# The last attention of a four-layer network begun among the last steps of the stage before it

## The chip, the cores and the metric

The kernel runs on one core of one Trainium2 chip. Its time is the device time of one execution in microseconds (us), given as the median of several runs. A profiled execution, taken separately, gives the trace from which single instructions are read.

The engines are named as in the profile: PE is TensorE (matrix products and transposes), PEld its weight loads, DVE is VectorE, ACT is ScalarE, POOL is GpSimd, and SP is SyncE, which here issues the DMAs. Every engine works through its own instructions in order; semaphores hold an instruction until what it needs is there. PSUM, in which TensorE leaves its results, has eight banks.

## The reference, cut to what matters

A tensor x of 16 tiles of 128 rows by 256 columns passes through four layers. Each layer adds an attention over a context (2048 rows) and then a feed-forward, each on the layer-normed x:

```python
x = x + L0_xattn(layernorm(x), ctx);        x = x + L0_ffn(layernorm(x))   # experts
x = x + L1_xattn(layernorm(x), ctx, mask);  x = x + L1_ffn(layernorm(x))   # ternary weights
x = x + L2_xattn(layernorm(x), ctx);        x = x + L2_ffn(layernorm(x))   # top four of 64 routes
x = x + L3_xattn(layernorm(x), ctx);        x = x + L3_ffn(layernorm(x))   # experts
```

The two parts that the change touches are these:

```python
def L2_ffn(x, A, B, W, bias):
    vecs = einsum('arh,bsh->bsar', A, x)             # 64 vectors of 16 per row
    routes = one_hot(top4(norm(vecs))).sum(-2) / 4
    v = einsum('bsa,bsar->bsr', routes, vecs)
    return x @ W.T + bias + einsum('bsa,ajr,bsr->bsj', routes, B, v)

def L3_xattn(x, cond, Wq, bq, Wkv, bkv, Wp, bp):      # 16 heads of 16
    q = (x @ Wq + bq) / 4;  k, v = split(cond @ Wkv + bkv)
    q, k, v = int8_roundtrip(q), int8_roundtrip(k), int8_roundtrip(v)
    attn = uint8_roundtrip(softmax(q @ k.T))          # over all 2048 rows of the context
    return (attn @ v) @ Wp + bp
```

## The kernel before, in words

`run` has four stages: the loading of x, the first layer (`l0`), the middle, and the last layer (`l3`).

**The middle** does layers 1 and 2, and the keys and values of layer 3, tile by tile. Each piece of work on one tile is a Python generator that yields between its steps: `l1_xattn`, `l1_ffn`, `l2_xattn`, `l2_ffn`, `l3_keys`, `l3_values`. The dictionary `starts` says at which step a generator begins (for tile t: 4t, 4t + 3, 4t + 7, 4t + 16, 4t + 2; the values at 4), and `side_by_side` advances all live generators in turn. The engines' final instruction order is made from this by the framework's scheduler.

Each generator belongs to a *stream*, which sets the buffers and the PSUM tag that its matrix products use. The middle's eight banks are e = 1, w = 3, x = 2, av = 1, f = 1. Layer 1 (streams `s1x`, `s1f`) takes tag e; layer 2's feed-forward (`s2f`) takes f, and so do keys and values (`s3`); layer 2's attention (`s2x`) takes x. With one bank behind e or f, each user waits until the one before it has been read out.

The steps of `l2_ffn`, whose last two tiles (14 and 15) end the middle: the layernorm (L187 to L193), its transpose (L213, copied at L229), `vecs` (L237, eight matmuls into two banks of tag w), their squares (L762, L763), the top four (L765 to L771), z and v (L776 to L781), the transposes of z (L213, L221), `out` (L237, 4 + 16 matmuls), and the addition to x (L787).

**The last layer** is a `tc.manual_schedule`: the order on every engine is the order in which the code stands. A unit u is one head of one tile, 256 in all. For each unit, `scores` makes four pieces of 128x512 (L933), `peak` their maxima (L939), `bias` the exponent's bias (L944, L945), and `exponentials` four exponentials into p (L955), after which SP issues one DMA that transposes p (L959); four units later (LAG) `values` multiplies it with the values (L967). Three buffers hold p (pool `l3p`), five its transpose. Scores of the units u + 1 and u + 2 are made while u is exponentiated.

Work per tile hangs on the dictionary `steps`, counted from the tile's first unit: steps below zero prepare the next tile's queries (`stats`, `norm` L982, `turn_h` L988 and L990, `project_q` L1001, `quant_q` L1008 to L1018, `turn_q` L1025 to L1028), those from 20 on finish attention and run the feed-forward of ten experts. For tile 0 the steps below zero stand ahead of the loop. The quantised queries of a tile lie in one of two buffers `qTs`, block-diagonal by pairs of heads, whose zeros a memset lays at the start (L1162). `take` gives each product the bank that came free first, `give` returns it; at the start they are taken b0, b1 and so on in order.

Between the two, `moe_weights` loads the weights of the last feed-forward (`w_L_ffn_wgu` 3520 KB at L95, `w_L_ffn_wd` in two parts at L384 and L386, `w_L_ffn_gateT` at L95). SP issues them, as it does all transposes of p. `l3_weights`, called before the middle, makes the pool w3, which stays to the end; buffers are laid out in memory in the order in which pools are opened and tiles asked for, so what is loaded later may lie over what an earlier stage still reads, and then waits for it.

Of the kernel before, what the change touches and what calls it, by code (L numbers as in the profile page):

```python
# [18 lines left out]
F32 = mybir.dt.float32  # L19
BF16 = mybir.dt.bfloat16  # L20
# [5 lines left out]
ALU = mybir.AluOpType  # L26
AX = mybir.AxisListType
PSUM = bass.MemoryType.PSUM

P = 128  # L30
NT = 16
D = 256
NH = 16
T = NT * P

MAGIC = 12582912.0
# [4 lines left out]
class Net:  # L41
# [767 lines left out]
    def l3_weights(self):  # L809

        w = {n: self.load(f"L3_xattn_{k}", [P, 2, D], f"x3{n}", "(c p) n -> p c n", p=P)
             for n, k in (("q", "Wq"), ("o", "Wp"))}
        w["qb"], w["ob"] = self.rows("L3_xattn_bq", "x3qb"), self.rows("L3_xattn_bp", "x3ob")
        w["k"] = [self.w.tile([P, 8, T // 2], BF16, name=f"kst{j}", tag=f"kst{j}") for j in range(2)]
        w["v"] = self.w.tile([P, NT, D], BF16, name="v_int", tag="v_int")
        w["sv"] = self.w.tile([P, 2], F32, name="sv", tag="sv")
        return w

    def l3_kv_weights(self):
# [28 lines left out]
    def l3_values(self, w, w3, pool):  # L848
# [18 lines left out]
        for j in range(8):  # L867
# [8 lines left out]
                nc.tensor.transpose(ps[:, i, :], vi[:, i, :], self.identb)  # L876
            nc.scalar.copy(w3["v"][:, t:t + 4, oc * P:(oc + 1) * P], ps)

    def middle(self, w3):

        self.tag = "e"
        w1f = self.w1f
        with (self.psum(e=1, w=3, x=2, av=1, f=1), self.stream("x1", bufs=1, small=2, tag="e", side="right") as s1x,
              self.stream("f1", bufs=1, small=2, tag="e", side="right") as s1f, self.pool("w2", 1) as self.w,
              self.stream("kv", bufs=1, small=2, tag="f") as s3, self.stream("x", bufs=1, small=2) as s2x,
              self.stream("f", bufs=1, small=2) as s2f):
            w2x, w2f, w3k = self.l2_xattn_weights(), self.l2_ffn_weights(), self.l3_kv_weights()
            starts = {}
            for t in range(NT):
                for step, st, make in ((0, s1x, lambda p, t=t: self.l1_xattn(t, p)),  # L890
                                       (3, s1f, lambda p, t=t: self.l1_ffn(t, w1f, p)),
                                       (7, s2x, lambda p, t=t: self.l2_xattn(t, w2x, p)),
                                       (16, s2f, lambda p, t=t: self.l2_ffn(t, w2f, p)),
                                       (2, s3, lambda p, t=t: self.l3_keys(t, w3k, w3, p))):
                    starts.setdefault(4 * t + step, []).append((st, make))
            starts[4].append((s3, lambda p: self.l3_values(w3k, w3, p)))
            self.side_by_side(starts)
        self.tag, self.small = None, self.small0

    def l3(self, w3, moe_w):  # L900
# [7 lines left out]
        nc, tc = self.nc, self.tc  # L908
        qw, ow, qb, ob, kst, v, sv = (w3[n] for n in ("q", "o", "qb", "ob", "k", "v", "sv"))
# [4 lines left out]
        with (self.pool("l3x", bufs=2) as pool, self.pool("l3p", bufs=3) as pp,  # L914
              self.pool("l3t", bufs=LAG + 1) as tp, self.pool("l3m", bufs=1) as mp,
              self.pool("l3e", bufs=3) as ep):
            st = {}

            banks = {f"b{j}": float(j - 7) for j in range(7)}

# [9 lines left out]
            def scores(u, q):  # L930
                t, hd = divmod(u, NH)
                ps, tag = st["s", u, q] = take([P, 512], "piece")
                nc.tensor.matmul(ps, qTs[t % 2][:, hd, :],  # L933
                                 kst[q // 2][:, hd // 2, 512 * (q % 2):512 * (q % 2) + 512], start=True, stop=True)

            def peak(u, q):
                if q == 0:
                    st["nm", u] = self.s(4, "nm")
                nc.vector.tensor_reduce(st["nm", u][:, q:q + 1], st["s", u, q][0], AX.X, ALU.max, negate=True)  # L939

            def bias(u):
                t, hd = divmod(u, NH)
                nb = st["nb", u] = self.s(1, "nb")
                nc.vector.tensor_reduce(nb, st.pop(("nm", u)), AX.X, ALU.min)  # L944
                nc.vector.tensor_scalar(nb, nb, st["sq", t][:, hd:hd + 1], LN255, ALU.mult, ALU.add)  # L945

            def exponentials(u):
                t, hd = divmod(u, NH)
                if hd == 0:
                    st["z", t] = pool.tile([P, NH, 4], F32, name="z", tag="z")  # L950

                p, nb = pp.tile([P, T], I16, name="p", tag="p"), st.pop(("nb", u))
                for q in range(4):
                    ps, tag = st.pop(("s", u, q))
                    nc.scalar.activation(p[:, 512 * q:512 * q + 512], ps, AF.Exp, bias=nb,  # L955
                                         scale=st["sq", t][:, hd:hd + 1], accum_out=st["z", t][:, hd, q:q + 1])
                    give(tag, u + 0.2 * (q + 1))
                pT = st["pT", u] = tp.tile([P, NT, P], I16, name="pT", tag="pT")
                nc.sync.dma_start_transpose(pT, p)  # L959

            def values(u):
                t, hd = divmod(u, NH)
                if hd == 0:
                    st["av", t] = self.bank([P, NH, 16], "av", "av")
                pb = st.pop(("pT", u)).bitcast(F16)
                for c in range(NT):
                    nc.tensor.matmul(st["av", t][:, hd, :], pb[:, c, :], v[:, c, hd * 16:(hd + 1) * 16],  # L967
                                     start=(c == 0), stop=(c == NT - 1))
# [159 lines left out]
            def down(k):  # L1128
                def step(t, u):
# [7 lines left out]
                    if k == 3:  # L1137
# [6 lines left out]
            steps = {-16: [stats], -15: [norm], -14: [turn_h], -13: [project_q], -12: [quant_q], -6: [turn_q],  # L1144
                     20: [divide], 21: [turn_o], 22: [project_o],
                     23: [stats_m], 24: [norm_m], 25: [turn_m], 27: [logits], 28: [top], 29: [combine]}
# [6 lines left out]

            N = NT * NH
            act = mp.tile([P, 14 * P], F32, name="act", tag="act")


            qTs = [mp.tile([P, NH, P], BF16, name=f"qT{j}", tag=f"qT{j}") for j in range(2)]
            with tc.manual_schedule(engines={E.PE, E.DVE, E.Activation, E.Pool, E.SP}):
                nc.gpsimd.memset(act[:, NE * IN:], 0.0)  # L1160
                for qT in qTs:
                    nc.gpsimd.memset(qT, 0.0)  # L1162
                for n in sorted(n for n in steps if n < 0):
                    for f in steps[n]:
                        f(0, -1)
                for q in range(4):
                    scores(0, q)
                    peak(0, q)
                bias(0)
                for q in range(2):  # L1170
                    scores(1, q)
                    peak(1, q)
                for u in range(N + 29):
                    if u < N:
                        exponentials(u)
                    if u + 1 < N:
                        for q in (2, 3):
                            scores(u + 1, q)
                            peak(u + 1, q)
                        bias(u + 1)  # L1180
                    later = []
                    for t in range(NT):
                        for f in steps.get(u - NH * t, ()) if u - NH * t >= 0 or t > 0 else ():
                            later.append(f(t, u))
                    if 0 <= u - LAG < N:
                        values(u - LAG)
                    for q in range(2):
                        if u + 2 < N:
                            scores(u + 2, q)
                    if u + 2 < N:  # L1190
                        peak(u + 2, 0)
                    for f in later:
                        if f:
                            f()
                    if u + 2 < N:
                        peak(u + 2, 1)
# [83 lines left out]
```

## Time and profile before

| what | value |
|---|---|
| median of 3 runs | 2981.75 us (2979.78 to 2983.23) |
| profiled execution: its time | 2974.05 us |
| its span in the trace | 2972.3 us |
| granted TensorE clock, mean | 0.931 |
| busy share PE, DVE, ACT, POOL | 82%, 66%, 59%, 34% |
| first layer, by the trace | up to about 1148 us |
| middle | about 1148 to 1827 us |
| last layer's first exponential | 1841.31 us |

The profiled execution's time holds 1.75 us that lie around the span. Times in the timeline are counted from the span's start; a row gives start, length, engine, line, operation, and in brackets how long the engine was idle before and what ended that. PEclk is the granted share of TensorE's full clock. Busy shares over the whole span mix four stages that have different limits, so a change at one place has to be read from the rows of that place.

### The profile page before, as it was taken

Reading aid. Unit: us, or ns where it says so; the run is one execution under the profiler, and the core shown is the slowest. Engines: PE = TensorE matmul, PEld = TensorE weight load, DVE = VectorE, ACT = ScalarE, POOL = GpSimd, SP = SyncE. Lnnn points to the kernel's source line nnn. Section 1 sums busy time; section 2 is a strip of 40 time slices with the busy share of each in tenths; the row PEclk is TensorE's granted clock in tenths of the full one; section 3 lists DMA queues with packets and bytes.
Section 4 is the critical chain, followed back from the end, with each engine's and each line's share of the span. In section 5 each row is a group of like instructions: output and inputs, shape, how many; then the busy total and the mean of one; then the engine's idle time right before and its main releaser. Section 6 shows DMA issues by size and latency. Waiting matters only on the chain. (4 is left out here: it accounts for less than half of the span.)

```text
span 2972.3 us, 41664 instructions
## 1 busy us (share of the span) xinstructions
PE 2438.9 (82%) x14053; PEld 1544.4 (52%) x14070; DVE 1958.2 (66%) x5045; ACT 1753.9 (59%) x4636; POOL 997.9 (34%) x1587
## 2 busy tenths in 40 slices
PE   4789999999999877788888885777777777777778
PEld 2456666666666544455555552344444444444445
DVE  2455566665666634577666644987877887877874
ACT  1234444444444432555555542988888888888884
POOL 2444444444443322555555531111111111121101
PEclk9999999999999998999999996699998999999999
DMA  5000000000000011000000003876666666666662
GB/s 208 1 1 1 1 1 1 1 1 1 1 1 36 23 44 32 5 5 5 5 5 5 1 1 99 155 132 121 126 123 123 123 124 123 128 124 118 125 124 56
DMA packets 559830, 171.38 MB, mean 58 GB/s; under 512 B 538912, under 2 KB 555904, under 8 KB 558848
## 3 DMA queue, kind: packets, MB, share of 16 engines
q1 hardware_dynamic: 559616, 168.72, 28.0%
q8 instruction: 111, 1.82, 0.2%
q14 instruction: 103, 0.84, 0.1%
HBM read 32.37 MB, written 2.10 MB: 12 GB/s over the span
## 5 line engine op out<-in xcount | busy, mean ns | idle before, releaser
L955 ACT ACTIVATE p<-piece,nb,hs 128x512 int16<-128x512 f32 x1024 | 785.2, 791 | 27.4 <-issue 17.2
L939 DVE TENSOR_REDUCE nm<-piece 128x1 f32<-128x512 f32 x1024 | 651.9, 683 | 111.0 <-PE piece L933 103.1
L933 PE MATMUL piece<-kst,qT 128*128 128x512 bf16 x1023 | 368.0, 415 | 201.4 <-DVE ma L1116 88.4
L1117 POOL TENSOR_TENSOR act<-ma,mb 128x176 f32<-128x176 f32 x160 | 88.9, 557 | 764.3 <-DVE ma L1116 763.9
L237 PE MATMUL gu<-w_L_ffn_wgu,mhT 128*128 128x352 f32 x640 | 255.1, 528 | 11.4 <-ACT p L955 8.0
L229 ACT COPY pT<-tp 128x512 f32<-128x512 f32 (+1 forms) x208 | 116.6, 563 | 199.8 <-PE tp L213 198.3
L933 PEld LDWEIGHTS <-qT 128*128 128x128 bf16 x1024 | 77.1, 98 | 298.3 <-issue 169.1
L955 ACT ACTIVATION_READ_ACCUMULATOR p<-piece,nb,hs 128x1 f32 x1024 | 222.6, 217 | 0.0
L263 POOL TENSOR_TENSOR kx<-kT,hmask 128x512 f32<-128x512 f32 x128 | 132.8, 1043 | 193.7 <-PE scores L266 122.1
L237 PEld LDWEIGHTS gu<-w_L_ffn_wgu,mhT 128*128 128x128 f32 x640 | 125.4, 209 | 132.7 <-ACT p L955 83.7
L268 DVE TENSOR_REDUCE mx<-scores 128x4 f32<-128x512 f32 x128 | 88.1, 689 | 157.1 <-PE scores L266 156.8
L967 PEld LDWEIGHTS <-pT 128*128 128x128 f16 x4096 | 144.0, 99 | 82.3 <-issue 67.5
L527 ACT ACTIVATE s<-s,nb,qs 128x128 f32<-128x128 f32 x256 | 123.2, 482 | 87.6 <-DVE nb L525 87.5
L282 PEld LDWEIGHTS av<-v,pT 128*128 128x128 f32 x1024 | 134.1, 199 | 77.2 <-ACT pT L229 66.6
L237 PE MATMUL gu<-w_L_ffn_wgu,hT 128*128 128x352 f32 x512 | 173.6, 461 | 0.5
L273 ACT ACTIVATE p<-scores,mx,qs 128x128 f32<-128x128 f32 x256 | 96.9, 459 | 121.3 <-DVE mx L271 113.2
L282 PE MATMUL av<-v,pT 128*128 128x17 f32 x1024 | 134.5, 263 | 40.8 <-ACT pT L229 40.8
L967 PE MATMUL av<-v_int,pT 128*128 128x16 bf16 x4096 | 143.3, 171 | 19.2 <-DVE o L1038 19.2
L266 PE MATMUL scores<-kx,qT 128*128 128x512 f32 x256 | 150.5, 672 | 2.3 <-ACT qT L229 1.8
L542 PE MATMUL oproj<-w_L_ffn_oT,oT 128*128 128x256 f32 x512 | 129.0, 396 | 4.0 <-ACT oT L536 3.9
L237 PE MATMUL q<-w_L_ffn_qT,hT 128*128 128x512 f32 x256 | 127.6, 599 | 2.3 <-DVE rot L481 2.0
L1136 PE MATMUL moe<-w_L_ffn_wd,aT 128*128 128x256 f32 x448 | 124.5, 426 | 3.6 <-ACT p L955 3.6
(362 smaller groups left out, 5271.4 us busy)
## 6 DMA issues: line engine op xcount, KB each, us to landing
pT<-p SPq DMA_TRANSPOSE x256, 4.3
w_L_ffn_wgu<-in_L_ffn_wgu SPq DMA_DIRECT2D x1, 3520.0 KB, 11.9
w_L_ffn_wgu<-in_L_ffn_wgu SPq DMA_DIRECT2D x1, 2816.0 KB, 9.5
x<-in_x SPq DMA_DIRECT2D x16, 128.0 KB, 4.8
ctxT<-in_ctxT SPq DMA_DIRECT2D x4, 512.0 KB, 5.4
w_L_ffn_qT<-in_L_ffn_qT SPq DMA_DIRECT2D x1, 2048.0 KB, 11.3
w_L_ffn_oT<-in_L_ffn_oT SPq DMA_DIRECT2D x1, 2048.0 KB, 16.2
ctx<-in_ctx SPq DMA_DIRECT2D x16, 128.0 KB, 2.0
```

The source lines that it names most:

```text
L229: nc.scalar.copy(out[:, j0:j0 + m, :], ps)
L237: self.nc.tensor.matmul(ps, a, b, start=(j == 0), stop=(j == n - 1))
L263: nc.gpsimd.tensor_tensor(kx, kT[oc].unsqueeze(1).to_broadcast([P, 4, P]), self.hmask[:, hs].unsqueeze(2).to_broadcast([P, 4, P]), ALU.mult)
L266: nc.tensor.matmul(ps, qT[:, oc, :], kx, start=True, stop=True)
L282: nc.tensor.matmul(av[:, 4 * g + h, :], pT[:, h, :], v[:, 4 * g + h, :], start=True, stop=True)
L527: nc.scalar.activation(s[:, j, :], s[:, j, :], AF.Exp, bias=nb[:, j:j + 1], scale=qs[:, j:j + 1], accum_out=z[:, j:j + 1])
L542: nc.tensor.matmul(proj, oT[:, j, :], w["o"][:, c, :], start=(c == 0), stop=(c == 15))
L933: nc.tensor.matmul(ps, qTs[t % 2][:, hd, :], kst[q // 2][:, hd // 2, 512 * (q % 2):512 * (q % 2) + 512], start=True, stop=True)
L939: nc.vector.tensor_reduce(st["nm", u][:, q:q + 1], st["s", u, q][0], AX.X, ALU.max, negate=True)
L955: nc.scalar.activation(p[:, 512 * q:512 * q + 512], ps, AF.Exp, bias=nb, scale=st["sq", t][:, hd:hd + 1], accum_out=st["z", t][:, hd, q:q ...
L967: nc.tensor.matmul(st["av", t][:, hd, :], pb[:, c, :], v[:, c, hd * 16:(hd + 1) * 16], start=(c == 0), stop=(c == NT - 1))
L1136: nc.tensor.matmul(ps, st["aT", k][:r, j, :], wd[:r, c, :], start=(c == 0), stop=(c == 13))
```

## The change

It has four parts. `l3_weights` asks for one more tile, qT0 (4 KB per partition), in the pool that stays open. A new generator `l3_first`, started at step 4 NT + 2 on stream `s1x` (bank e), makes the queries of tile 0 among the middle's last steps, in buffers of the keys' stream. The feed-forward of tile 15 in layer 2 uses bank e in place of f. And the last layer begins with `scores` of unit 0: it finds the queries and their scales in w3, clears one query buffer in place of two, and lays its banks by empty allocations in the order b6, b3, b4, b5, av, b0, b1, b2, so that b0, which is taken first, and its followers fall on other banks of the middle than before.

```diff
@@ l3_weights
         w["sv"] = self.w.tile([P, 2], F32, name="sv", tag="sv")
+        w["qT"] = self.w.tile([P, NH, P], BF16, name="qT0", tag="qT0")
         return w
@@
+    def l3_first(self, w3, kv_pool, pool):
+        nc = self.nc
+        nc.gpsimd.memset(w3["qT"], 0.0)
+        h = self.layernorm(0, pool)
+        yield
+        hT = self.transposed(h, 2, pool, "hT")
+        ps = self.mm([P, D], "q")
+        self.matmul_acc(ps, [(hT[:, c, :], w3["q"][:, c, :]) for c in range(2)])
+        q = kv_pool.tile([P, D], F32, name="k", tag="k")
+        nc.vector.tensor_tensor(q, ps, w3["qb"], ALU.add)
+        yield
+        v = q.rearrange("p (h d) -> p h d", d=16)
+        am, s4, r, sq = (self.small0.tile([P, NH], F32, name=n, tag=f"{n}{NH}") for n in ("ham", "hs4", "hr", "hs"))
+        nc.vector.tensor_reduce(am, v, AX.X, ALU.max, apply_absolute_value=True)
+        nc.vector.tensor_scalar(s4, am, 1.0 / 127.0, 4e-8, ALU.mult, ALU.max)
+        nc.vector.reciprocal(r, s4)
+        nc.vector.tensor_scalar(sq, s4, 0.25, None, ALU.mult)
+        nc.gpsimd.tensor_tensor(v, v, r.unsqueeze(2).to_broadcast([P, NH, 16]), ALU.mult)
+        nc.gpsimd.tensor_scalar(q, q, MAGIC, None, ALU.add)
+        qi = kv_pool.tile([P, NH, 64], BF16, name="parts", tag="parts")
+        nc.gpsimd.memset(qi[:, :, 48:], 0.0)
+        for j in range(3):
+            nc.gpsimd.tensor_scalar(qi[:, :, 16 * j:16 * j + 16], v, -MAGIC, None, ALU.add)
+        yield
+        ps = self.tp([P, 8, P], "htp", BF16)
+        for j in range(8):
+            nc.tensor.transpose(ps[:, j, :], qi[:, 2 * j:2 * j + 2, :].rearrange("p h d -> p (h d)"), self.identb)
+        out = w3["qT"].rearrange("p (j two) q -> p j two q", two=2)
+        nc.scalar.copy(out[:64, :, 0, :], ps[:64])
+        nc.vector.tensor_copy(out[64:, :, 1, :], ps[64:])
+        w3["sq"] = sq
@@ middle
             w2x, w2f, w3k = self.l2_xattn_weights(), self.l2_ffn_weights(), self.l3_kv_weights()
+            last = s2f[:2] + ("e",)
...
-                                       (16, s2f, lambda p, t=t: self.l2_ffn(t, w2f, p)),
+                                       (16, last if t == NT - 1 else s2f, lambda p, t=t: self.l2_ffn(t, w2f, p)),
...
             starts[4].append((s3, lambda p: self.l3_values(w3k, w3, p)))
+            starts.setdefault(4 * NT + 2, []).append((s1x, lambda p: self.l3_first(w3, s3[0], p)))
             self.side_by_side(starts)
@@ l3
-            st = {}
+            st = {("sq", 0): w3["sq"]}
+            for tag in ("b6", "b3", "b4", "b5", "av", "b0", "b1", "b2"):
+                self.bank([P, 512], tag, "none")
...
-            qTs = [mp.tile([P, NH, P], BF16, name=f"qT{j}", tag=f"qT{j}") for j in range(2)]
+            qTs = [w3["qT"], mp.tile([P, NH, P], BF16, name="qT1", tag="qT1")]
             with tc.manual_schedule(engines={E.PE, E.DVE, E.Activation, E.Pool, E.SP}):
                 nc.gpsimd.memset(act[:, NE * IN:], 0.0)
-                for qT in qTs:
-                    nc.gpsimd.memset(qT, 0.0)
-                for n in sorted(n for n in steps if n < 0):
-                    for f in steps[n]:
-                        f(0, -1)
+                nc.gpsimd.memset(qTs[1], 0.0)
                 for q in range(4):
                     scores(0, q)
                     peak(0, q)
```

## The prediction

> **What bounds the kernel now.** The page first, for the slices (74.3 us each): VectorE and ScalarE at eight tenths after slice 25, and a hole before it.
>
> ```profile
> PE   4789999999999877788888885777777777777778
> DVE  2455566665666634577666644987877887877874
> ACT  1234444444444432555555542988888888888884
> PEclk9999999999999998999999996699998999999999
> ```
>
> Attention (1838 to 2918 us) is bound by the exponentials on ScalarE, one unit each 3.05 us; the change adds nothing there. Slice 24 is the seam that it edits. The table by stretch shows the seam's engines:
>
> ```profile
> core 0: us, PE busy (x) PEld busy (x) DVE busy (x) ACT busy (x) POOL busy (x), PEclk, DMA share, GB/s
> 1735.00:1790.00 55.00, 41.76 (x198) 28.39 (x196) 26.69 (x63) 22.23 (x56) 14.56 (x24) 0.94 0.00 1
> 1790.00:1803.00 13.00, 8.67 (x28) 6.49 (x28) 0.79 (x3) 1.17 (x2) 1.92 (x1) 0.62 0.00 0
> 1803.00:1827.00 24.00, 12.63 (x38) 8.01 (x38) 6.84 (x16) 2.74 (x5) 6.21 (x6) 0.72 0.38 149
> 1827.00:1838.00 11.00, 2.63 (x15) 1.81 (x17) 2.20 (x7) 1.38 (x2) 4.44 (x7) 0.67 0.52 167
> ```
>
> From 1790 on no engine is full: it is a chain of single steps, so a step removed is worth its whole length, and one moved ahead of 1735 goes where TensorE has 13 us idle in 55. The timeline names the chain:
>
> ```profile
> 1798.04 4.58 PE L237 MATMUL out<-w_L_ffn_B,zT 128*128 128x256 f32 x16
> 1803.13 0.44 PE L213 MATMUL tp<-ident,ln_h 128*128 128x128 f32 x2 [0.52 <-DVE x L787]
> 1804.03 3.70 PE L237 MATMUL vecs<-w_L_ffn_AT,hT 128*128 128x512 f32 x8 [0.46 <-ACT hT L229]
> 1822.31 4.39 PE L237 MATMUL out<-w_L_ffn_B,zT 128*128 128x256 f32 x16
> 1827.08 0.40 DVE L982 TENSOR_SCALAR ln_h<-x,ln_mv,ln_r 128x256 f32<-128x256 f32 x1
> 1828.44 1.13 PE L237 MATMUL q<-w_L_xattn_Wq,hT 128*128 128x256 f32 x4 [0.46 <-ACT hT L990]
> 1832.85 2.48 POOL L1018 TENSOR_SCALAR qi<-q 128x256 bf16<-128x256 f32 x3
> 1835.39 1.04 PE L1025 MATMUL htp<-identb,qi 128*128 128x128 bf16 x8 [5.82 <-POOL qi L1018]
> 1837.98 2.77 PE L933 MATMUL piece<-kst,qT 128*128 128x512 bf16 x6 [1.55 <-ACT qT L1027]
> 1841.31 0.78 ACT L955 ACTIVATE p<-piece,nb,hs 128x512 int16<-128x512 f32 x1 [3.79 <-DVE nb L945]
> ```
>
> Tile 15's feed-forward waits at 1803.13 for tile 14's result, since both hold bank f (its ln_h had been ready since 1786.85). After the last `out` (E = 1826.70) come ten dependent steps to the first exponential, E+14.61. On SP the weights of the last feed-forward come before the transposes of p:
>
> ```profile
> 1116.91 0.37 SPq L95 DMA_DIRECT2D w_L_xattn_Wkv<-in_L_xattn_Wkv  x1
> 1158.84 1.01 PE L806 MATMUL htp<-identb,parts 128*128 128x128 bf16 x8 [6.21 <-DVE qs L245]
> 1816.78 0.38 SPq L95 DMA_DIRECT2D w_L_ffn_wgu<-in_L_ffn_wgu  x1
> 1818.43 8.77 SPq L95 DMA_DIRECT2D w_L_ffn_gateT<-in_L_ffn_gateT  x1
> 1844.49 31.46 SPq L959 DMA_TRANSPOSE pT<-p  x10
> ```
>
> **The change part by part.**
>
> *1. Queries taken off the seam.* After `out`(15) the changed order has scores(0,·) at once. Left in the chain: 4 scores pieces with their maxima, nb, the first exponential. In the trace that is from 1837.98 to 1841.31, 3.33 us; with 0.22 us of hand-over the exponential comes at E+3.55 instead of E+14.61: **−11.06**. The banks are laid so that scores(0,·) meet those freed early (tags e, f, w first); none waits for the last x add, 0.42 us. The two memsets of qT (3.54 us, POOL) ran beside out(15), worth nothing; the one left runs there too.
>
> *2. The same work put in at 1735 to 1752.* TensorE gets ln_h's transposes 0.38, q 1.13, htp 1.0 = 2.5 us; POOL 0.62 + 0.86 + 2.48 (its memset earlier); DVE 0.42+0.42+0.17+0.25+0.17+0.69 = 2.1; ScalarE 0.38 + 1.01. TensorE works in order, so htp waits there for POOL's three qi parts (done about 1748), and behind it stand the q projection of the second layer's tile 15 and its scores; ScalarE's copy into qT stands ahead of that tile's kT. Walking these queues, the scores of tile 15 (1751.83) come **3.3 later**. Floor 0 (it fits into the 13 us of idle TensorE), ceiling 5.3, POOL's and ScalarE's parts end to end. From there the last tile's attention is a chain up to z(14), so I carry all of it.
>
> *3. Tile 15 in bank e.* In the new order tile 15's ln_h transpose and the first quarter of `vecs` (3.70 / 4 = 0.92 us each) run before z(14) is transposed, quarters two and three between z's two transposes and `out`, where TensorE is idle anyway, then out(14), then quarter four. If the middle quarters fit, out(14) ends as before at 1802.62 and `vecs` at 1803.54 instead of 1807.73: **−4.2**. Should they push (0.92 in idle times of 0.68, twice), it is −3.7. What follows (squares, top four, z, out) is unmoved. With part 2: E comes **−0.9** (−4.2 if part 2 is free, +2 if it costs its ceiling and the vecs gain is smaller).
>
> *4. The weights of the last feed-forward.* qT0's 4 KB per partition, in a pool opened before the middle, shift all buffers opened later, so wgu now lies over memory that the last `out` still reads: its load waits for E, where before it waited only for POOL's z (1816.75, E−9.9). Queued behind it on SP: both wd, gateT, and every pT. In the trace gateT's issue ends 10.4 us after wgu's start and the last of these lands 17.1 us after. So now: SP free at E+10.4, data until E+17.1. pT(0) is due at E+6.7 (3.55 + a unit) and takes 2.6 to 3.7 us of its own once the weights are through: E+19.7 to E+20.8. p has three buffers, so exponential 3, due at about E+13, waits for pT(0): **+6.7 to +7.8; I take 7**. In before, the same queue was empty by E+7.2, ahead of the first pT at E+17.8. Up to 1.5 comes back (the stall covers ScalarE's idle of 1.02 at 1858.03 and 0.52 at 1861.70, both in before's first units); I take 0.5. Start of attention: −11.06 + 7 − 0.5 = **−4.6**.
>
> Here a rule matters. The row is gateT's 8.77 us of issue[...]. The Trainium skill, "DMA: Bandwidth & Descriptors", section "Queues, rings and completion order", says that engines take turns between queue rows, but that all of one issuer's descriptors lie on one ring per engine and are consumed in order. By the rule pT(0) moves no byte before the weights' 17.1 us are over: 7. If turns were taken among the queued transfers, only the held issue would count: pT(0) out at E+10.4, landing 4.3 later (the page's median), E+14.7, a stall of 1.7. No row of before has a transpose behind a load; I go with the rule.
>
> *5. The first 155 us of the middle.* The same shift makes Wkv wait for the last gate/up matmul of the first layer's experts (ends 1140.24) instead of 1116.9, so it lands near 1145, and the instruction order of TensorE from 1148 to 1303 (554 instructions) is another: the second layer's first chain goes ahead (its first gate matmul, 1163.25, about 6 earlier, into the 6.21 us of idle before htp), the keys of tile 0 come 13 to 16 later. From 1303 to 1735 the order is the same, and by work both orders have met again by about 1221. I take **−1**, between −6 (the idle gained for good) and +8 (half of the keys' delay kept).
>
> *The clock.* Granted was 0.62 to 0.72 in the seam, and out's 16 matmuls took 4.58 there against 3.62 at 1772. The Trainium skill, "TensorE: Matmul & The Clock Gate", "Part 1: The HAM clock gate (the "warmup" mystery)", puts the clock at half after one idle window of about 3.4 us. Part 3 closes some gaps, which by the rule could warm out(14) or out(15), another −1 to −1.8; the gap from 1807.73 to 1816.81 (top four and z) remains ahead of out(15), so I take the rows: 0.
>
> **Sum:** −1 (5) − 0.9 (2 and 3) − 4.6 (1 and 4) = −6.5 us. It stands against the profiled execution: span 2972.3, 2974.05 with the 1.75 around it, so 2967.5. That execution is 7.70 below the median 2981.75; carried over, the median comes to 2975.2, about 2975 (−0.22%). A difference of 0.2%, 5.96 us, is about what a measurement of this kernel can tell from no change.
>
> **The rivals.**
> *A. The transposes are not held.* The weights let pT through early: stall 0 to 2. For it: DMA share is only 0.52 in the seam. Against: gateT's blocked issue. Then −1 − 0.9 − 11.06 + 0 to 1.7: −11 to −13, about 2969.
> *B. Little is left.* The stall is 8 to 10, since the DMA share is 0.93 at 1870 to 1900 and a queue of transposes drains slowly; and part 3 does not do what it says (the fourth quarter behind out(14) holds the chain, and only the transpose and its copy, 0.9 of the 4.2, are won). Each alone leaves −3 to −5; together −1 + 2.4 − 11.06 + 9 = −0.7: about 2981.
> *C. Slower: bank f holds the middle's start.* Keys and values share one bank f with the fourth chain's feed-forward. With the keys begun 13 to 16 later, feed-forwards queue behind them and the delay stays to the end. It decides from δ = +11.6 in part 5 (net over +5.96); at +14 the net is +8.4: about 2990. For it: one bank, in-order TensorE. Against: 37 tenants in 155 us at about 2.7 us each (k 1.03 and add 0.42, htp 1.01 and copy about 1, with hand-over) need only 100 us.
>
> **How the numbers follow.** The forecast's case (−3 to −10) 0.45, A 0.17, B 0.22, C 0.16. The forecast's own range is 2972 to 2979. Over 0.2% faster: 0.27 of the forecast's 0.45 plus A, 0.44. Slower by as much: C and a crumb of B, 0.17. Between: 0.39. The range 2967 to 2988 takes in A, B and the lower half of C, and leaves out C's upper half and a warm clock on top of A.
>
> **What would show it.** The first exponential 3.5 us after the last `out` (part 1); ScalarE idle of about 7 us ahead of the fourth unit, released by the DMA, with wgu issued at E (4); none of it is A. ln_h(15)'s transpose ahead of out(14), and E about 1 earlier against 1735 (2, 3). The first gate matmul earlier than 15.0 us after the first keys matmul, and the stretch to 1303 within 4 us of before (5); if that is over 11 longer, C. A wait for POOL at TensorE near 1748 longer than 3.3 us, or another change within attention (2918−1841), would make the forecast wrong.

## The result, and the profile after

The change made the kernel slower: 2987.30 us against 2980.59 (medians of ten runs each, 2981.25 to 2995.48 and 2976.17 to 2983.23), a ratio of 1.0022, 95% interval 1.0011 to 1.0032. That is +6.7 us where −6.5 was forecast. The profiled execution has a span of 2984.9 us against 2972.3, +12.6; it is near its own median (2986.61 us), while that of before was faster than all ten of its runs (2974.05), so part of the 12.6 is chance and has to be told from the rest.

The slices of the page after show the end of the first layer and the middle's start at a lower granted clock (from about 970 to 1340 us, at 74.6 us a slice) and the hole at the seam narrower:

```profile
PE   4789999999999877888888886777777777777778
ACT  1334444444444432555555542898888888888885
PEclk9999999999999887889999997588999899999999
```

Landmarks read from the two timelines say where the time went. z(t) is the start of GpSimd's last product for z (L781) in layer 2's feed-forward of tile t. Each row is a stretch between two of them (us):

| stretch | before | after | difference |
|---|---|---|---|
| to the last `moe` matmul of the first layer | 1148.17 | 1155.28 | +7.1 |
| from there to z(2) | 213.85 | 227.44 | +13.6 |
| z(2) to z(12) | 371.13 | 371.25 | +0.1 |
| z(12) to the end of the last `out` (E) | 93.55 | 95.47 | +1.9 |
| E to the first exponential | 14.61 | 3.33 | −11.3 |
| first exponential to the 13th (unit 3) | 9.48 | 15.45 | +6.0 |
| from there to the end | | | −4.8 |

The seam did what the prediction said. In the timeline after, the first pieces follow the last `out` at once, and the exponential comes 3.33 us after E (L976, L998 and L1002 are L933, L955 and L959 of before):

```profile
1843.70 5.75 PE L237 MATMUL out<-w_L_ffn_B,zT 128*128 128x256 f32 x16
1849.29 1.67 PE L976 MATMUL piece<-kst,qT 128*128 128x512 bf16 x7
1849.58 0.38 SPq L95 DMA_DIRECT2D w_L_ffn_wgu<-in_L_ffn_wgu  x1
1851.23 8.39 SPq L95 DMA_DIRECT2D w_L_ffn_gateT<-in_L_ffn_gateT  x1
1852.78 0.78 ACT L998 ACTIVATE p<-piece,nb,hs 128x512 int16<-128x512 f32 x1 [11.00 <-DVE nb L988]
1859.66 21.00 SPq L1002 DMA_TRANSPOSE pT<-p  x6
1868.23 0.78 ACT L998 ACTIVATE p<-piece,nb,hs 128x512 int16<-128x512 f32 x1 [5.85 <-DMA pT<-p]
```

The weights go out at E, the first transpose is issued when gateT's issue is over, and ScalarE waits 5.85 us for it.

The loss is at the start of the middle. Here are the two stretches up to z(0) and z(2), of before and then of after (columns: length, then busy time and count for PE, PEld, DVE, ACT, POOL, then granted clock, DMA share, GB/s):

```profile
1148.17:1284.08 135.91, 105.11 (x470) 61.06 (x473) 81.60 (x242) 70.67 (x167) 73.24 (x115) 0.92 0.02 5
1284.08:1362.02 77.94, 64.92 (x339) 45.26 (x340) 54.25 (x153) 42.85 (x109) 45.23 (x72) 0.96 0.02 4
```

```profile
1155.28:1300.12 144.84, 112.16 (x460) 66.48 (x459) 83.26 (x240) 69.65 (x164) 72.41 (x114) 0.84 0.02 5
1300.12:1382.72 82.60, 68.89 (x354) 47.83 (x352) 54.33 (x153) 43.99 (x111) 46.15 (x73) 0.94 0.01 4
```

TensorE does about as many matmuls (809 and 814 are recorded) and is busy 181.05 us instead of 170.03: of the 13.6 us, 11.0 are longer matmuls, at a clock of 0.84 instead of 0.92 in the first stretch. The clock fell after TensorE's waits. These are its longest from 1148 to 1384 us (total, times, longest), of before and then of after:

```profile
PE htp L806 <- DVE qs L245: 6.2, 1, 6.2
PE tp L213 <- DVE a L687: 4.5, 3, 3.7
```

```profile
PE tp L213 <- DVE a L687: 11.7, 2, 8.2
PE htp L806 <- DVE sm L678: 5.2, 1, 5.2
```

and in the timeline after, where the new order has nothing to put into the longest of them:

```profile
1147.37 0.37 SPq L95 DMA_DIRECT2D w_L_xattn_Wkv<-in_L_xattn_Wkv  x1
1164.66 0.60 PE L237 MATMUL gate<-tern_gate,hT 128*128 128x512 bf16 x2 [0.57 <-ACT hT L219]
1167.86 1.03 PE L237 MATMUL k<-w_L_xattn_Wkv,ctxT 128*128 128x256 f32 x4
1177.10 1.09 PE L213 MATMUL tp<-ident,a 128*128 128x128 f32 x4 [8.21 <-DVE a L687]
1183.84 1.06 PE L806 MATMUL htp<-identb,parts 128*128 128x128 bf16 x8
```

After before's wait of 6.2 us the granted clock was 0.50 for 6 us; after the one of 8.2 us it was 0.50 for 12 us, with TensorE at work in most of them (before's row first), and after the one of 5.2 us 0.59 for another 5.

```profile
1159.00:1165.00 6.00, 5.11 (x17) 2.33 (x17) 0.47 (x3) 2.43 (x4) 0.31 (x1) 0.50 0.00 0
```

```profile
1177.00:1189.00 12.00, 9.47 (x33) 5.84 (x34) 6.11 (x19) 3.02 (x5) 5.47 (x10) 0.50 0.04 11
```

The waits that the profile puts down to `qs` and `sm` are those of `htp`, which reads the keys' `parts`; `qs` and `sm` are merely the instructions that follow on VectorE (the last piece of `parts` was done at 1158.69 and at 1209.28, `htp` began at 1158.84 and 1209.34).

Of the +7.1 before that, about 1.5 belongs to the change. The scheduler put `l3_first`'s memset of qT0 into the first layer, beside VectorE's `hn` of the last tile, for which TensorE waits. `hn` took 1.86 us instead of 0.35, before's row first:

```profile
1116.49 0.35 DVE L554 TENSOR_SCALAR hn<-hid,n 128x256 f32<-128x256 f32 x1 [1.77 <-POOL n L182]
```

```profile
1121.78 1.80 POOL L885 MEMSET qT<- 128x2048 bf16 x1
1121.87 1.86 DVE L554 TENSOR_SCALAR hn<-hid,n 128x256 f32<-128x256 f32 x1 [1.78 <-POOL n L182]
```

In all three versions with this memset there (after, and after_ms and after_kvfirst below) this `hn` took 1.86 us, in the other ten traces 0.34 to 0.35.

The rest of the +7.1 I take for chance. Apart from that memset and two loads that SP issues later, every engine has the same instructions in the same order through the first layer. About half of it comes where the same four matmuls, with the same wait ahead of them, meet a granted clock of 0.54 instead of 1.00, before's row first:

```profile
1004.20 1.98 PE L237 MATMUL k<-w_L_ffn_kvT,hT 128*128 128x512 f32 x4 [0.44 <-DVE hT L224]
```

```profile
1004.60 3.51 PE L237 MATMUL k<-w_L_ffn_kvT,hT 128*128 128x512 f32 x4 [0.44 <-DVE hT L224]
```

Of the versions below, six (noshift, noshift_f, early54, early54_f, bank_e, noshift_ms) have exactly before's orders on every engine and on SP in this layer, and in their traces it ends at 1156.6, 1147.8, 1153.0, 1154.8, 1148.1 and 1156.4 us.

### The profile page after: what moved, and what is told of

Same layout as the page of the kernel before. It is cut to its first block, busy times and chain, and to the rows that moved or that the text cites. A ratio compares the mean times of both kernels' runs of the same rounds, so it can differ in the third digit from the quotient of the medians.

```text
span 2984.9 us, 41665 instructions
## 1 busy us (share of the span) xinstructions
PE 2455.5 (82%) x14070; PEld 1553.8 (52%) x14070; DVE 1962.1 (66%) x5046; ACT 1753.4 (59%) x4636; POOL 999.7 (33%) x1586
## 5 line engine op out<-in xcount | busy, mean ns | idle before, releaser
L998 ACT ACTIVATE p<-piece,nb,hs 128x512 int16<-128x512 f32 x1024 | 785.2, 791 | 40.5 <-issue 17.3
L976 PE MATMUL piece<-kst,qT 128*128 128x512 bf16 x1024 | 367.4, 414 | 205.7 <-DVE ma L1159 88.2
L976 PEld LDWEIGHTS <-qT 128*128 128x128 bf16 x1024 | 77.1, 98 | 296.0 <-issue 167.6
L998 ACT ACTIVATION_READ_ACCUMULATOR p<-piece,nb,hs 128x1 f32 x1024 | 222.7, 218 | 0.0
L542 PEld LDWEIGHTS oproj<-w_L_ffn_oT,oT 128*128 128x128 f32 x512 | 98.3, 198 | 48.2 <-ACT oT L536 29.6
## 6 DMA issues: line engine op xcount, KB each, us to landing
w_L_ffn_wgu<-in_L_ffn_wgu SPq DMA_DIRECT2D x1, 3520.0 KB, 11.6
w_L_ffn_qT<-in_L_ffn_qT SPq DMA_DIRECT2D x1, 2048.0 KB, 10.4
```

Source lines behind the costliest of these rows:

```text
L542: nc.tensor.matmul(proj, oT[:, j, :], w["o"][:, c, :], start=(c == 0), stop=(c == 15))
L976: nc.tensor.matmul(ps, qTs[t % 2][:, hd, :], kst[q // 2][:, hd // 2, 512 * (q % 2):512 * (q % 2) + 512], start=True, stop=True)
```

## The experiments

Ratios are against the kernel before, run on the same chip. Names such as noshift are used in what follows.

**1. The shift alone**: before, with an unused tile where qT0 stands.

```diff
         w["sv"] = self.w.tile([P, 2], F32, name="sv", tag="sv")
+        w["qT"] = self.w.tile([P, NH, P], BF16, name="qT0", tag="qT0")
+        self.nc.gpsimd.memset(w["qT"][:, 0, 0:2], 0.0)
```

> The kernel before with one unused tile of 4 KB per partition in the pool w3 (a few elements of it are cleared by GpSimd) and nothing else of the change. Theory 1 (the shift of the buffers, by the other instruction order that it brings at the start of the middle, costs the time): slower than before by 12 to 16 us, about 2994; tile 0's first route product z later by 12 or more than the end of the first layer is. Theory 2 (what the trace of after shows there is the clock gate's phase, chance): within 3 us of before. Theory 3 (half and half): +5 to +9.

2994.01 us against 2980.52, ratio 1.0041 (1.0028 to 1.0053): +13.5. From the first layer's end to z(2) its trace takes 228.57 us, before 213.85. A tile that nobody uses costs all that the change lost. Theory 1 stands.

**2. The shift with Wkv loaded first**, which brings TensorE's order near that of before: of before's 238 runs of like matmuls up to z(2), 9 stand elsewhere in the trace, instead of 149 with the shift alone.

```diff
-            w2x, w2f, w3k = self.l2_xattn_weights(), self.l2_ffn_weights(), self.l3_kv_weights()
+            w3k, w2x, w2f = self.l3_kv_weights(), self.l2_xattn_weights(), self.l2_ffn_weights()
```

> The same unused tile, and Wkv loaded ahead of the other weights of the middle, so that it overwrites memory that is free early; TensorE's order at the start of the middle is then nearly that of before. Theory 1 (the order, which follows the late Wkv): the loss goes, 0 to +4 us against before. A rival (the shift costs by the lateness of loads whatever the order): it stays at +10 or more, since other loads are then the late ones. Theory 2 (chance): within 3 us, as without it.

2983.74 us, ratio 1.0010 (1.0000 to 1.0019): +3.2 of the 13.5 stay. The stretch to z(2) takes 218.71 us. So some 10 us are the order that follows a late Wkv, not the shift as such; what the last 3 to 5 are is open (other loads are later, and the order is still not quite before's).

**3. The change without the shift** (noshift): tile 0's queries lie in half of one plane of ctxT, the columns of tiles 0 to 7, whose readers are done long before.

```diff
-        w["qT"] = self.w.tile([P, NH, P], BF16, name="qT0", tag="qT0")
+        w["qT"] = self.ctxT[:, 0, :1024].bitcast(BF16).rearrange("p (h q) -> p h q", q=P)
```

> The whole change, but tile 0's queries lie in the part of ctxT that nobody reads any longer instead of in a tile of their own, so that no buffer moves; loads and the order at the start of the middle are those of before. Theory 1: only the seam is left: 11.3 earlier at the first exponential after the last out, 2 to 3 given back in the last tiles, no hold of the transposes (the weights go out 10 us ahead of the last out again): 8 to 10 us faster than before, about 2971. Theory 2: the loss was not in the order, so the gain over the change as made is only the 6 us of held transposes: about before's time.

2970.79 us, ratio 0.9960 (0.9946 to 0.9974): −9.7. The stretch to z(2) is 213.94 us, before's again, although the first layer of this trace ended at 1156.6 us; so a late end of the first layer does not bring the loss that follows it. And unit 3's first exponential comes 9.48 us after the first, as in before, with no wait for a DMA. Both losses hung on the 4 KB.

**4. The same with tile 15's feed-forward back in bank f** (noshift_f: `last = s2f`).

> As noshift, with the last tile's feed-forward back in bank f. By the step of the prediction (its vecs 4.2 us earlier by the other bank): slower than noshift by about 4, that is 4 to 6 faster than before. Rival: the bank buys nothing, since z's transposes and out hold TensorE anyway: the same as noshift.

2981.64 us, ratio 0.9997 (0.9987 to 1.0006). The medians put 10.8 us between the two, which the traces don't: z(12) to E takes 96.54 us here and 95.46 in noshift. Eight of its 14 runs had a mean clock of 0.922 to 0.925, where noshift had 0.926 to 0.929 in all six. In the traces z(15) follows z(14) after 19.84 us with bank e and 25.29 with f, and with bank e most of that is lost again between z(12) and E: 1.7 us of it are slower matmuls in tile 14's `vecs` (5.38 us in noshift, 3.68 in noshift_f). This pair leaves open what the bank is worth.

**5. The bank again, from the other side**: before with the bank alone (bank_e), and a second pair with the queries begun at step 54 (early54, early54_f).

```diff
+            last = s2f[:2] + ("e",)
-                                       (16, s2f, lambda p, t=t: self.l2_ffn(t, w2f, p)),
+                                       (16, last if t == NT - 1 else s2f, lambda p, t=t: self.l2_ffn(t, w2f, p)),
```

> The kernel before with tile 15's second-layer feed-forward in bank e, nothing else. By the prediction's step: z(15) 4.2 us nearer to z(14) than before (20.0 instead of 24.2), and the whole about 4 us faster. By the medians of the versions without the shift (2971 against 2982 with bank f) it would be 10, which no step of the trace explains; if the trace is right, that difference is mostly the clock gate's and this run shows 2 to 5.

2963.99 us against 2981.53, ratio 0.9950 (0.9936 to 0.9964). All three guesses were too low, by the medians (17.5) and by the trace: z(15) comes 10.79 us after z(14) instead of 24.21, E 13.58 earlier. The timeline shows another order than the change has:

```profile
1786.38 0.41 DVE L193 TENSOR_SCALAR ln_h<-x,ln_mv,ln_r 128x256 f32<-128x256 f32 x1 [0.72 <-POOL ln_r L182]
1787.02 1.29 DVE L776 TENSOR_TENSOR z<-vecs,routes 128x512 f32<-128x512 f32 x2
1788.00 6.22 PE L237 MATMUL vecs<-w_L_ffn_AT,hT 128*128 128x512 f32 x8 [0.46 <-ACT hT L229]
1790.56 1.92 POOL L781 TENSOR_TENSOR z<-routes,v 128x1024 f32<-128x1024 f32 x1 [2.96 <-DVE v L780]
1797.69 3.62 PE L237 MATMUL out<-w_L_ffn_B,zT 128*128 128x256 f32 x16
1801.35 1.92 POOL L781 TENSOR_TENSOR z<-routes,v 128x1024 f32<-128x1024 f32 x1 [8.86 <-PE out L237]
```

All of tile 15's `vecs` stand ahead of z(14)'s transposes, and its squares, top four and v run on ScalarE and VectorE under out(14). In the change one quarter is behind out(14), and all of that comes after it:

```profile
1812.67 1.29 DVE L776 TENSOR_TENSOR z<-vecs,routes 128x512 f32<-128x512 f32 x2
1813.88 0.40 DVE L193 TENSOR_SCALAR ln_h<-x,ln_mv,ln_r 128x256 f32<-128x256 f32 x1
1815.48 2.07 PE L237 MATMUL vecs<-w_L_ffn_AT,hT 128*128 128x512 f32 x2 [0.46 <-ACT hT L229]
1824.67 3.62 PE L237 MATMUL out<-w_L_ffn_B,zT 128*128 128x256 f32 x16
1828.13 1.02 PE L237 MATMUL vecs<-w_L_ffn_AT,hT 128*128 128x512 f32 x2
1836.22 1.92 POOL L781 TENSOR_TENSOR z<-routes,v 128x1024 f32<-128x1024 f32 x1 [17.94 <-DVE v L780]
```

VectorE's ln_h of tile 15 has slipped behind z(14)'s two products, and everything with it.

> The version without the shift, with tile 0's queries begun at step 54 instead of 66, among full steps of the middle. If the 2.4 us that they cost at 1735 to 1752 come from the last tiles being a chain, they cost less there: 1 to 2 us faster than the version without the shift, and tile 13's z no later against tile 12's than before. Rival: TensorE is 86 per cent busy in the middle, so 2.5 us of its work cost 2.5 us anywhere: the same, only earlier.

> As early54, with the last tile's feed-forward in bank f: a second measure of what the bank is worth. By the trace 2 to 4 us slower than early54; by the medians of the first pair 10 us slower.

2971.99 us (ratio 0.9974, 0.9962 to 0.9986) and 2975.76 us (0.9986, 0.9977 to 0.9994). With step 54, z(13) stays with z(12) (30.48 us after it; before 30.77, noshift 33.16), so the 2.4 us that the queries cost among the last tiles do go; the median against noshift tells nothing (2972.0 and 2970.8). The bank is worth 3.8 us here by the medians (the two intervals overlap), and 6.0 by the traces from z(12) to E (89.64 against 95.65).

**6. The memset between z(13) and z(14).** In the change GpSimd clears the second query buffer between z(13) and z(14); in before its two memsets (3.54 us at 1816.76) come after z(15). The row after:

```profile
1801.87 1.81 POOL L1202 MEMSET qT<- 128x2048 bf16 x1 [6.98 <-PE tp L213]
```

With that buffer in ctxT as well, cleared in `l3_first`, the scheduler puts all of tile 15's `vecs` ahead again. (The edit takes away the memset and the buffer's own tile together; which of the two sets the order is not separated.) This was tried on the change as made (after_ms), on noshift (noshift_ms) and on early54 (early54_ms).

```diff
+        w["qT1"] = self.ctxT[:, 1, :1024].bitcast(BF16).rearrange("p (h q) -> p h q", q=P)
...
         nc.gpsimd.memset(w3["qT"], 0.0)
+        nc.gpsimd.memset(w3["qT1"], 0.0)
...
-            qTs = [w3["qT"], mp.tile([P, NH, P], BF16, name="qT1", tag="qT1")]
+            qTs = [w3["qT"], w3["qT1"]]
...
-                nc.gpsimd.memset(qTs[1], 0.0)
```

> The change as made, with the second query buffer also laid in a part of ctxT that nobody reads any longer and cleared in l3_first; so the memset of 1.81 us leaves GpSimd's queue between z(13) and z(14), and the scheduler then sets all four quarters of tile 15's vecs ahead of z(14). The theory from the run with the bank alone (in before's order the bank is worth 13.5, in the changed order only 4.3 less the insertion): z(15) about 11 us after z(14) instead of 19.9, 8 to 10 faster than the change as made, about 2978. Rival (the bank's gain in that run was the clock's luck): no more than 2 faster.

2981.37 us against 2982.77, ratio 0.9991 (0.9978 to 1.0004), against 1.0022 for the change as made: some 9 us better relative to before, with wide scatter (2970.7 to 2990.0). The trace is plainer: z(15) comes 9.69 us after z(14), after 19.87 in the change.

> The same with tile 0's queries in ctxT too, so that no buffer moves: the bank in full (13.5), the queries off the seam (11.1), less 2.4 for the insertion: 20 to 24 faster than before, about 2958, if the parts add. Rival (they meet again at the weights of the last feed-forward: issued 10 us ahead of an earlier out, they hold the first transposes): 14 to 18 faster, with ScalarE idle ahead of the fourth unit.

2960.90 us, ratio 0.9930 (0.9917 to 0.9944): 21.9 us faster than before, the lowest ratio here (its interval overlaps that of bank_e), and at the seam the parts add:

```profile
1805.09 5.24 PE L237 MATMUL vecs<-w_L_ffn_AT,hT 128*128 128x512 f32 x8 [0.46 <-ACT hT L229]
1807.83 1.93 POOL L781 TENSOR_TENSOR z<-routes,v 128x1024 f32<-128x1024 f32 x1 [2.90 <-DVE v L780]
1817.45 1.92 POOL L781 TENSOR_TENSOR z<-routes,v 128x1024 f32<-128x1024 f32 x1 [7.69 <-PE out L237]
1819.39 0.38 SPq L95 DMA_DIRECT2D w_L_ffn_wgu<-in_L_ffn_wgu  x1
1824.01 4.25 PE L237 MATMUL out<-w_L_ffn_B,zT 128*128 128x256 f32 x16
1831.59 0.78 ACT L1000 ACTIVATE p<-piece,nb,hs 128x512 int16<-128x512 f32 x1 [9.50 <-DVE nb L990]
```

z(12) to E is 80.08 us (before 93.55), and E to the first exponential 3.33 (before 14.61): 24.8 us. Unit 3 is 9.48 us after it, so weights issued 8.9 us ahead of E hold no transpose; that rival falls.

The memsets moved into the middle are not free, though. Beside the two of them, two short instructions of VectorE took 3.31 us each; in before they took 0.22 and 0.28.

```profile
1446.33 1.80 POOL L886 MEMSET ctxT<- 128x2048 bf16 x1
1446.60 3.31 DVE L271 TENSOR_SCALAR mx<-mx,qs 128x4 f32<-128x4 f32 x1
1446.73 3.31 DVE L845 CAST parts<-k 128x256 bf16<-128x256 f32 x1
```

From z(2) to z(12) it is 377.90 us here and 378.69 in early54_ms, 371.98 to 375.27 in the five versions with one such memset in that stretch, and 371.12 to 372.34 in the six traces with none. How much of this is the memsets and how much the clock is not separated.

> As the last one, with the queries begun at step 54. z(13) stays with z(12) as in the earlier run with step 54: 1 to 2 us faster than the last one, within what these runs can tell.

2966.76 us, ratio 0.9944 (0.9929 to 0.9959). Not faster than noshift_ms. In the trace z(13) does stay with z(12) (30.48 us after it, 33.01 in noshift_ms), and z(12) to E is 1.4 us shorter; the stretch to z(2) is 2.3 longer, and attention after unit 3 is 7.2 longer, where the two programs are the same. The gain is below what such stretches scatter.

**7. The change with Wkv first**: the late order mended, the held transposes left.

> The change as made, with Wkv loaded ahead of the other weights of the middle; the tile qT0 and its shift stay, TensorE's order at the start of the middle is again nearly that of before, and the weights of the last feed-forward still wait for the last out. Theory 1 (the order costs about 10, the held transposes 6): 8 to 11 faster than the change as made, 3 to 5 slower than the version without the shift: about 2977, 3 to 5 faster than before, with ScalarE held about 6 us ahead of the fourth unit. Rival (the shift costs through its memory waits, whatever the order): no faster than 2984.

2978.34 us, ratio 0.9988 (0.9980 to 0.9995), 3.2 faster than before. ScalarE's wait is still there:

```profile
1851.32 0.78 ACT L998 ACTIVATE p<-piece,nb,hs 128x512 int16<-128x512 f32 x1 [5.78 <-DMA pT<-p]
```

So the two costs of the 4 KB come apart: about 10 for the order, 6 for the weights.

## Why the prediction was right or wrong, point by point

*Part 5, the first 155 us of the middle: wrong, and it decided the sign.* The step that failed is that "by work both orders have met again by about 1221". Taking off the 7.1 us of the first layer, the first gate matmul did come 5.7 us earlier, and tile 0's keys 12.5 and its htp 17.9 later, as read from the order. But the third tile's gate (1221.1 in before) came 8.7 later, the fifth 13.3, and the lead was never made up. I compared the work in the two orders at one clock and without their waits. In fact the order leaves TensorE waiting 8.2 and 5.2 us, with the work that could fill the time behind the waiting instruction, and the matmuls after ran slower: 11.0 of the 13.6 us. I took −1, between −6 and +8; the shift alone measured +13.5 in the median, +14.7 in the trace to z(2).

*The memset of qT0: put at nothing.* The prediction has "its memset earlier" and gives it no cost; in the first layer it held VectorE's `hn`, about 1.5 us.

*Rival C.* Its size and sign are what happened (it decides from +11.6; its own terms give about +11.5), but its mechanism was not seen. The longest wait is for VectorE's `a` of the second layer's first tile, in bank e; the next is for the keys' `parts`, and whether bank f had a share in it no run tests. That the total fell where C put it is luck as far as its reason goes.

*Part 1, queries off the seam: right.* −11.28 measured for −11.06.

*Part 4, the held transposes: right, 6.0 for 7.* wgu was issued 0.13 us after E, gateT's issue ended at E+10.2 (10.4 forecast), unit 3 began at E+18.8 (about 20 forecast). The 0.5 that I thought would come back did not: the waits of 1.12 and 0.53 us at the sixth and seventh groups of exponentials are there as in before. Rival A is out. The last of the weights landed at E+17.1, as forecast, and the first transpose 1.6 us after it, at E+18.7, where 2.6 to 3.7 were counted: that is the 6.0 instead of 7. The Trainium skill's "DMA: Bandwidth & Descriptors", section "Queues, rings and completion order", by which descriptors are consumed in ring order, led to the right side (not E+14.7). The trace doesn't show that this is the reason, since the transpose's own issue was held too, from E+10.2 to E+16.7.

*Part 2, the insertion: right in kind.* z(13) came 2.4 later relative to z(12), for 3.3.

*Part 3, the bank: the sum right, the reading short.* z(15) came 4.34 nearer to z(14), for 4.2. The order that I took as the only one wastes two thirds of the bank: bank_e has 13.4, and one memset with its buffer lies between the two (after_ms has 9.69 us where the change has 19.87). That was not in the prediction at all.

*The clock at 0: wrong by about 4.* In the change tile 14's `vecs` took 5.38 us (3.68 in before) and the last `out` 5.75 (4.39): z(14) 2.5 later (1.7 of it these `vecs`, the rest is open), E 1.4 later. So 2.4 + 2.5 − 4.3 + 1.4 makes the +1.9 of the tail, where −0.9 was forecast.

*What no part explains.* The −4.8 within attention. Between the same exponentials (unit 3 to the last) the other traces lie between −4.7 (shift_kvfirst) and +3.4 (early54_ms) against before; I take it for the clock's scatter, which is not shown.

The sum with what was measured, 1.5 + 13.6 + 0.1 + 1.9 − 11.3 + 6.0 = +11.8 of the trace, without the rest of the first layer (+5.6) and the −4.8, lies above the medians' +6.7 (by the interval, +3.3 to +9.5). Why is not shown.

## What to carry to other kernels

A tile that is asked for in a long-lived pool moves everything laid behind it. Compare not only the instructions that the change names but which old reader each load now waits for, and where the scheduler puts what depends on it; memory whose last reader is long done takes a small buffer without moving anything. When an order changes, don't compare the work in it: walk its waits on each in-order engine, and count the matmuls after a long wait at the lower clock. Look where the scheduler puts a memset that depends on nothing. And try each part of a change alone: here the part thought to be worth 4 us was worth 13 by itself, and another part's buffer and its memset hid it.

## What the runs showed of the hardware that was not expected

When the granted clock falls is worth more than most of the edits here: the same first layer ended anywhere from 1147.8 to 1156.6 us, four matmuls taking 1.98 or 3.51 us after the same wait, and 27 runs of the kernel before spread over 13.8 us (2973.12 at a mean clock of 0.932, 2986.94 at 0.927). A few runs of two versions can differ by 10 us with traces that agree to 1 us at the place of the edit (noshift and noshift_f), so a part is better judged by landmarks in the trace than by a few times.

A memset of 128x2048 on GpSimd (1.80 us) can hold VectorE for as long: `hn` took 1.86 us beside it instead of 0.35, `mx` and `parts` 1.56 beside one (noshift) and 3.31 beside two in a row (noshift_ms), instead of 0.22 and 0.28. It does not hold every instruction: a BATCH_NORM_STATS2 beside the one in the middle of after_ms took 0.38 us, as elsewhere.
